# Attention layer 1: two transposes of running maxima moved among the score matmuls, and the last two weight sums of a unit put on four column groups

## The chip, the cores and the metric

The kernel runs on one core of a Trainium2 chip. A core has five engines with one instruction queue each: PE (TensorE, matmuls and transposes into PSUM), DVE (VectorE), ACT (ScalarE), POOL (GpSimd) and SP, which here only issues DMAs. An engine executes its queue in order; engines wait for each other through semaphores. The metric is the device time of one execution in microseconds (us), the median of three runs.

## The reference

Two layers run one after the other on x of shape (2, 256, 64, 64). Layer 0 is a gated attention with heads of 16 channels. The change touches only layer 1, a plain attention over 4096 positions with four heads of 64 channels:

```python
qkv = jnp.einsum('oc,bchw->bohw', w_qkv, x) + b_qkv[None, :, None, None]
qkv = qkv.reshape(b, HEADS, 3 * head_dim, h * w)
q, k, v = jnp.split(qkv, 3, axis=2)
scale = 1.0 / jnp.sqrt(jnp.asarray(head_dim, x.dtype))
attn = jax.nn.softmax(jnp.einsum('bhdn,bhdm->bhnm', q, k) * scale, axis=-1)
out = jnp.einsum('bhnm,bhdm->bhnd', attn, v).reshape(b, c, h, w)
return jnp.einsum('oc,bchw->bohw', w_out, out) + b_out[None, :, None, None] + x
```

Everything is float32. The softmax needs, for each query, the maximum of its scores, the exponentials and their sum.

## The kernel before

Layer 1 is cut into 32 units (b, g, j): image b, pair of heads g, block j of 512 queries. A unit has 32 chunks m of 128 keys; one chunk of scores for both heads is a tile of 128 partitions (keys) by 1024 elements (two heads, 512 queries each). The chunks form two groups n of 16, and each group has its own maxima.

The main loop goes by steps t, two chunks per step and 16 steps per unit. In this text the steps of a unit are numbered 0 to 15 by the unit whose scores they compute. The scores of a chunk are kept raw in a ring of 26 buffers and used 11 or 12 steps later, when the maxima of its group are known. So one step holds, for two new chunks and two old ones:

- PE: `score` (line 888), two matmuls a chunk into one of two PSUM pair buffers; `gather` (1030), the product of the old chunks' weights with the values; and one of several side jobs: a quarter of a projection (812, 835), transposes of maxima (`turn_max`, 918), sums of weights (1043 and 1060), transposes of results (1085).
- DVE: the running maximum `rmax` (905) of each new chunk, and `shift` (977), which adds the negative maximum to each old chunk.
- ACT: a copy of the new scores into the ring (906, after the `rmax` of the same chunk), which frees the PSUM pair buffer for the score two chunks later; the exponential of the old chunks (`weigh`, 989); copies of side results out of PSUM.
- POOL: `acc` (999 and 1001), the sum over chunks of the weights, one addition of 128x1024 per chunk for 30 of 32 chunks. Chunk 11 of each group is shifted on POOL (966), not on DVE. A ring buffer comes free for a new chunk only when POOL has added the old one: the copy of chunk 9 of a unit takes the buffer of chunk 15 of the unit before, 26 chunks back.

`seq` records the order of the code as the order of each engine's queue, so the order of the calls in the loop at line 1364 is the order on the engines. Side jobs are hung on a step with a place, by `at(step, place, job)`, and called by `hung(step, place)`. The order of a step was: both scores, exponential of one old chunk, "start", "early", `keep` of the first new chunk (rmax and copy), shift and exponential of an old chunk, "early end", `keep` of the second, both gathers, "late", "late end", shift of the next old chunk, "end".

All PSUM side results share one bank, which `misc` hands out (tag `misc`, one buffer): who takes it waits until its last reader is done.

The parts that the change touches:

- Folding the maxima, at step 8 for the first group and at step 0 of the next unit for the second. `turn_max(u, n, k)` transposes the running maxima of head k (four 128x128 transposes) into the `misc` bank, and `fold` reduces them on DVE (935, `negs`) and sends them by DMA. Head 0 was turned "early" and folded "early end"; head 1 was turned "late" and folded "late end". Both heads use the one `misc` bank, so the second transpose needs the first reduction to be over.
- Projected values: `store_values` copies a half out of the `misc` bank on ACT at step 8 ("start"); in the last eight units `output` does the like (1200).
- The weights of chunks 30 and 31 are not added by POOL. `gather` sums them on PE at step 11 of the next unit, by matmuls with a block of ones (1043). Both chunks went to the same two column groups (partitions 64 and 96 of the tile `sum`), accumulating. At step 12 `total` (1060) added the two POOL sums, the first on partitions 0 and 32, the second again on 64 and 96. `keep_total` at step 13 copied the tile out (1068) and turned it to one value per query by four small DMAs to DRAM and one back; `add_sums` at step 15 combined the groups on POOL (1151, 1152), and `factors` the reciprocals.

Of the kernel before, what the change touches and what calls it, by code (L numbers as in the profile page):

```python
# [8 lines left out]
F32 = mybir.dt.float32  # L9
# [5 lines left out]
P = 128  # L15
# [5 lines left out]
D1 = 64  # L21
# [5 lines left out]
def conv_attention_kernel(  # L27
# [743 lines left out]
    with (  # L771
# [23 lines left out]
            (u, n): dram.tile([2, NB], F32, tag=f"neg_{u}_{n}", name=f"neg_{u[0]}{u[1]}{u[2]}_{n}")  # L795
            for u in units for n in range(NG)
        }
        sum1 = {
            u: dram.tile([NG * 2, NB], F32, tag="sum_{}_{}_{}".format(*u), name=f"sum_{u}")
            for u in units  # L800
        }
        first, begun, late = {}, set(), {}


# [217 lines left out]
        def gather(t):  # L1022
            u = b, g, j = units[t // NM]
            m = t % NM
            n = m // GS
            if m % GS == 0:
                avs1[u, n] = psv.tile([P, NB], F32, tag="av", name=f"av1_{b}_{g}_{j}_{n}")
            v = vs[b, g, m // PB]
            for k in range(2):
                seq(nc.tensor.matmul(  # L1030
                    avs1[u, n][k * D1 : (k + 1) * D1, :], v[:, m % PB, k, :], raws[t][:, k, :],
                    start=(m % GS == 0), stop=(m % GS == GS - 1),
                ))
            if on_tensor(t) and t % 2 == 1 and t != 2 * END - 1:
                late_sums((t - 1, t) if on_tensor(t - 1) else (None, t))
            elif t == 2 * END - 2:
                late_sums((t, t + 1))
            if m == NM - 1 and u != units[-1]:
                srows[u] = misc(f"sum1_{b}_{g}_{j}")
                for i in (t - 1, t):  # L1040
                    for k in range(2):
                        r = D1 * (NG - 1) + 32 * k
                        seq(nc.tensor.matmul(
                            srows[u][r : r + 32, :], ones[:, :32], raws[i][:, k, :],
                            start=(i < t), stop=False, skip_group_check=True,
                        ))
            raws.pop(t - 2, None)
            if m % GS == GS - 1:
                a = l1.tile([P, NB], F32, tag="avs", name=f"avs1_{b}_{g}_{j}_{n}")
                seq(nc.scalar.copy(a, avs1.pop((u, n))))  # L1050
                avs1[u, n] = a

        def total(u):


            b, g, j = u
            for n in range(NG):
                for k in range(2):
                    r = D1 * n + 32 * k
                    seq(nc.tensor.matmul(  # L1060
                        srows[u][r : r + 32, :], ones[:, :32], accs[u, n][:, k, :],
                        start=(n < NG - 1), stop=True, skip_group_check=True,
                    ))

        def keep_total(u):
            b, g, j = u
            row = l1.tile([P, NB], F32, tag="kv", name=f"srow_{b}_{g}_{j}")
            seq(nc.scalar.copy(
                row.rearrange("p (a m i) -> p a i m", m=P, i=2),
                srows[u].rearrange("p (a i m) -> p a i m", m=P, i=2),  # L1070
            ))
            for m in range(2 * NG):
                nc.sync.dma_start(out=sum1[u][m : m + 1, :], in_=row[32 * m : 32 * m + 1, :])
            s = small.tile([P, NG, 2, PB], F32, tag="sums1", name=f"sums1_{b}_{g}_{j}")
            nc.sync.dma_start(
                out=s.rearrange("p n k (a i) -> p (n k a) i", i=2),
                in_=sum1[u].rearrange("m (a p i) -> p (m a) i", p=P, i=2),
            )
            srows[u] = s
            seq(nc.scalar.activation(losts[u], losts[u], AF.Exp, scale=D1**-0.5))  # L1080

        def turned(a, name):
# [66 lines left out]
        def add_sums(u):  # L1149
            s, lost = srows[u], losts[u]  # L1150
            seq(nc.gpsimd.tensor_tensor(s[:, 0], s[:, 0], lost, ALU.mult))
            seq(nc.gpsimd.tensor_tensor(s[:, 1], s[:, 1], s[:, 0], ALU.add))

        def factors(u):
# [66 lines left out]

        for n, u in enumerate(units):
            b, g, j = u
            t0 = n * US
            if n > 0:
                at(t0 - 9, "start", lambda u=u, b=b, j=j: fetch(("q", u), x1[b][j]))
                for q in range(4):
                    at(t0 - (3, 3, 2, 2)[q], "late", lambda u=u, q=q: next_queries(u, q))  # L1230
                at(t0 - 2, "start", lambda u=u: keep_next_queries(u, 0))
                at(t0 - 1, "start", lambda u=u: keep_next_queries(u, 1))
            if n < len(units) - NJ:
                to = (*units[n + NJ][:2], j)
                at(max(t0 - 1, 0), "start", lambda to=to: fetch(("kv", *to), x1[to[0]][to[2]]))
                for q in range(4):
                    at(t0 + 2 + q, "late", lambda to=to, q=q: next_keys(*to, q))
                    at(t0 + (6, 7, 9, 10)[q], "late", lambda to=to, q=q: next_values(*to, q))
                at(t0 + 6, "start", lambda to=to: store_keys(*to))
                for i, step in enumerate((t0 + 8, t0 + 11)):  # L1240
                    at(step, "start", lambda to=to, i=i: store_values(*to, i))

                t1 = (n // NJ * NJ + NJ - 1) * US
                at(t1 + 2 * j + 2, "start", lambda to=to: load_keys(*to))
                at(t1 + 2 * j + 3 + LAG, "start", lambda to=to: load_values(*to))
            for k in range(NG):
                t1 = t0 + (k + 1) * GS // 2
                places = ("early", "early" if (u, k) == (units[-1], NG - 1) else "late")
                for i, place in enumerate(places):
                    at(t1, place, lambda u=u, k=k, i=i: turn_max(u, k, i))  # L1250
                    at(t1, f"{place} end", lambda u=u, k=k, i=i: fold(u, k, i))
                at(t1 + 2, "end", lambda u=u, k=k: place_shift(u, k))
            t1 = t0 + US + GS // 2
            if u != units[-1]:
                at(t1 + 4, "late", lambda u=u: total(u))
                at(t1 + 5, "start", lambda u=u: keep_total(u))
                at(t1 + 1, "late", lambda u=u: lose(u))
                at(t1 + 7, "late end", lambda u=u: add_sums(u))
                at(t1 + 8, "end", lambda u=u: factors(u))
                for place, k in (("early", 1), ("late", 0)):  # L1260
                    at(t1 + 9, place, lambda u=u, k=k: turn_sums(u, k))
                    at(t1 + 9, f"{place} end", lambda u=u, k=k: rows(u, k))
            else:
                at(END + 1, "late", lambda u=u: last_lost(u))
                at(END + 4, "early", lambda u=u: late_sums((None, None)))
                at(END + 4, "early end", lambda u=u: keep_late(0))
                at(END + 5, "early", lambda u=u: turn_late(0))
                at(END + 5, "early end", lambda u=u: add_late(u, 0))
                at(END + 6, "early", lambda u=u: turn_sums(u, 0))
                at(END + 6, "early end", lambda u=u: first_rows(u))  # L1270
                at(END + LAG, "late", lambda u=u: turn_late(1))
                at(END + LAG, "late", lambda u=u: add_late(u, 1))
                at(END + LAG, "late", lambda u=u: turn_sums(u, 1))
                at(END + LAG, "late", lambda u=u: last_rows(u))
            if n >= len(units) - NJ:
                b0 = B - 2
                at(t0 - 1, "start", lambda b0=b0, j=j: fetch_output(b0, j))
                for o in range(CC):
                    for q in range(4):
                        step = t0 + ((2, 3, 4, 5), (6, 7, 9, 10))[o][q]  # L1280
                        at(step, "late", lambda b0=b0, j=j, o=o, q=q: project_out(b0, j, o, q))
                at(t0 + 6, "start", lambda b0=b0, j=j: output(b0, j, 0, 2))
                for part, step in enumerate((t0 + 8, t0 + 11)):
                    at(step, "start", lambda b0=b0, j=j, part=part: output(b0, j, 1, part))

# [76 lines left out]
        for t in range(max(t for t, _ in extras) + 1):  # L1364
            inside, behind = 0 <= t < END, 0 <= t - LAG < END
            pair = (2 * t, 2 * t + 1)
            scores = [score(c) for c in pair] if inside else []
            if 0 <= t - LAG - 1 < END:
                weigh(pair[1] - 2 * LAG - 2)
            hung(t, "start")  # L1370
            hung(t, "early")
            if inside:
                keep(pair[0], scores[0])
# [83 lines left out]
```

## Time and profile before

| | value |
|---|---|
| median of 3 runs | 4638.63 us (4638.25 to 4638.99) |
| the profiled execution, its own time | 4640.95 us |
| its span, first to last instruction | 4639.2 us |
| PE, DVE, ACT, POOL busy in the span | 97%, 83%, 74%, 54% |
| one unit of layer 1, 3123.58 to 3202.48 us | 78.90 us |
| in it PE, DVE, ACT, POOL busy | 75.83, 73.99, 69.75, 74.19 us |
| mean granted TensorE clock | 0.996 |

Layer 1 begins near 2070 us; its units follow each other at 78.9 us (79.0 in the last eight). In a unit four engines are each busy for 88 to 96% of the time, so no single share tells what bounds it. The page counts time to the modelled end of a matmul, which overlaps the next; the distance from one start to the next start on an engine is the time that an instruction takes of its queue, and the prediction goes by that.

The timeline has one line per run of equal instructions: start in us, length in us, engine, line, operation, output and inputs, shapes, how many, and in square brackets the idle time before it and what ended it. Each fp32 matmul shows as two instructions, so a chunk of scores is "x4".

### The profile page before, as it was taken

Reading aid. Unit: us, or ns where it says so; the run is one execution under the profiler, and the core shown is the slowest. Engines: PE = TensorE matmul, PEld = TensorE weight load, DVE = VectorE, ACT = ScalarE, POOL = GpSimd, SP = SyncE. Lnnn points to the kernel's source line nnn. Section 1 sums busy time; section 2 is a strip of 40 time slices with the busy share of each in tenths; the row PEclk is TensorE's granted clock in tenths of the full one; section 3 lists DMA queues with packets and bytes.
Section 4 is the critical chain, followed back from the end, with each engine's and each line's share of the span. In section 5 each row is a group of like instructions: output and inputs, shape, how many; then the busy total and the mean of one; then the engine's idle time right before and its main releaser. Section 6 shows DMA issues by size and latency. Waiting matters only on the chain. (4 is left out here: it accounts for less than half of the span.)

```text
span 4639.2 us, 73122 instructions
## 1 busy us (share of the span) xinstructions
PE 4499.0 (97%) x28490; PEld 1511.6 (33%) x28490; DVE 3833.4 (83%) x4443; ACT 3439.9 (74%) x4588; POOL 2514.8 (54%) x1307
## 2 busy tenths in 40 slices
PE   8999999999999999999999999999999999999998
PEld 3433333333333333333333333333333333323332
DVE  6777777777777777529999999999999999999997
ACT  3266666666666666668888888888888888888885
POOL 5300000000000000008999999999999999999995
PEclk9999999999999999999999999999999999999999
DMA  3100000000000000121111221111211112111213
GB/s 101 39 4 20 20 20 15 15 15 15 15 15 15 15 13 13 33 75 40 35 42 35 55 56 39 37 40 42 71 42 36 39 33 62 51 53 37 53 40 112
DMA packets 190475, 174.84 MB, mean 38 GB/s; under 512 B 120232, under 2 KB 121064, under 8 KB 190128
## 3 DMA queue, kind: packets, MB, share of 16 engines
q1 hardware_dynamic: 188272, 169.58, 13.2%
q8 instruction: 223, 3.65, 0.3%
q14 instruction: 124, 1.02, 0.1%
q10 hardware_dynamic: 1856, 0.59, 0.1%
HBM read 127.65 MB, written 42.48 MB: 37 GB/s over the span
## 5 line engine op out<-in xcount | busy, mean ns | idle before, releaser
L1001 POOL TENSOR_TENSOR acc<-acc,raw 128x1024 f32<-128x1024 f32 x821 | 1950.4, 2376 | 80.1 <-ACT raw L989 30.7
L402 DVE TENSOR_REDUCE mx<-a 128x1 f32<-128x512 f32 x2048 | 1315.5, 686 | 449.9 <-PE a L398 448.8
L439 ACT ACTIVATE p<-s 128x512 f32<-128x512 f32 x2048 | 1108.3, 595 | 702.5 <-PE a L398 367.6
L905 DVE TENSOR_TENSOR rmax<-s,rmax 128x1024 f32<-128x1024 f32 x960 | 1171.6, 1220 | 99.7 <-PE s L888 89.6
L436 PE MATMUL s<-q,kT 32*128 32x512 f32 x4096 | 1218.8, 640 | 0.0
L888 PE MATMUL s<-q,k 64*128 64x512 f32 x4096 | 1120.3, 637 | 98.1 <-ACT raw L906 93.2
L906 ACT COPY raw<-s 128x1024 f32<-128x1024 f32 x1024 | 1035.6, 1011 | 240.8 <-DVE rmax L905 163.5
L977 DVE TENSOR_TENSOR raw<-raw,shift 128x1024 f32<-128x1024 f32 x961 | 1160.7, 1212 | 3.3 <-ACT shift L959 1.8
L989 ACT ACTIVATE raw<-raw 128x1024 f32<-128x1024 f32 x1024 | 1084.9, 1060 | 62.8 <-DVE raw L977 27.7
L398 PE MATMUL a<-kT,q 32*128 32x512 f32 x4096 | 1129.8, 643 | 1.4 <-DVE mx L402 1.3
L1030 PE MATMUL av<-raw,v 128*64 128x512 f32 x4096 | 1007.4, 607 | 4.2 <-ACT raw L989 2.5
L451 PE MATMUL av<-p,v 128*32 128x256 f32 (+1 forms) x7904 | 650.1, 399 | 0.6 <-ACT avs L465 0.6
L501 POOL TENSOR_TENSOR f<-f,dyn 128x16 f32<-128x16 f32 x15 | 3.3, 221 | 1028.2 <-DVE f L500 1028.2
L888 PEld LDWEIGHTS s<-q,k 64*128 64x128 f32 x4096 | 316.8, 185 | 678.7 <-ACT raw L906 487.0
L436 PEld LDWEIGHTS s<-q,kT 32*128 32x128 f32 x4096 | 397.7, 183 | 426.3 <-issue 392.1
L1030 PEld LDWEIGHTS av<-raw,v 128*64 128x64 f32 x4096 | 242.4, 136 | 650.8 <-issue 476.4
L451 PEld LDWEIGHTS av<-p,v 128*32 128x32 f32 x7904 | 157.7, 108 | 751.5 <-issue 737.3
L552 POOL TENSOR_SCALAR res<-res 128x1024 f32<-128x1024 f32 x16 | 16.7, 1044 | 660.3 <-ACT res L551 660.3
L398 PEld LDWEIGHTS a<-kT,q 32*128 32x128 f32 x4096 | 305.2, 184 | 31.4 <-DVE mx L402 18.2
L999 POOL TENSOR_TENSOR acc<-raw,raw 128x1024 f32<-128x1024 f32 x64 | 152.1, 2376 | 60.9 <-ACT raw L989 60.3
L966 POOL TENSOR_TENSOR raw<-raw,row 128x1024 f32<-128x1024 f32 x63 | 151.7, 2407 | 37.9 <-DMA row<-neg 37.9
L935 DVE TENSOR_REDUCE negs<-rt 128x4 f32<-128x512 f32 x126 | 87.0, 690 | 58.8 <-PE rt L918 58.8
(338 smaller groups left out, 1913.5 us busy)
## 6 DMA issues: line engine op xcount, KB each, us to landing
row<-neg SPq DMA_DIRECT2D x64, 512.0 KB
x<-in_x_dram SPq DMA_DIRECT2D x16, 512.0 KB
res<-in_x_dram SPq DMA_DIRECT2D x16, 512.0 KB
x<-res SPq DMA_DIRECT2D x16, 512.0 KB
att<-rows SPq DMA_DIRECT2D x62, 128.0 KB
kd<-k1s SPq DMA_DIRECT2D x24, 256.0 KB
vd<-v1s SPq DMA_DIRECT2D x24, 256.0 KB
k<-kd SPq DMA_DIRECT2D x24, 256.0 KB
```

The costliest lines, as they stand in the source:

```text
L398: seq(nc.tensor.matmul(ps, qs0[u][r, bass.ts(i, P)], kTs[b][r, bass.ts(m, NB)], start=True, stop=True,))
L402: seq(nc.vector.tensor_reduce(mxs[u][:, i * H + h, m : m + 1], ps, AX.X, ALU.max))
L436: seq(nc.tensor.matmul(ps, kTs[b][r, bass.ts(m, P)], qs0[u][r, :], start=True, stop=True))
L439: seq(nc.scalar.activation(pt[:, k, :], ps, AF.Exp, scale=D0**-0.5))
L451: seq(nc.tensor.matmul(avs[u][32 * h : 32 * h + 32, cols], vs0[b][:, m, 32 * h : 32 * h + 32], pts[t, h // 2][:, h % 2, cols], start=(m == ...
L888: seq(nc.tensor.matmul(ps[:, k, :], ks[b, g, m // PB][r, bass.ts(m % PB, P)], qs1[u][r, :], start=True, stop=True,))
L905: seq(nc.vector.tensor_tensor(rmax[u, n], ps, before, ALU.max))
L906: seq(nc.scalar.copy(raw, ps))
L977: seq(nc.vector.tensor_tensor(raws[t], raws[t], shifts[u, t % NM // GS], ALU.add))
L989: seq(nc.scalar.activation(p, p, AF.Exp, scale=D1**-0.5))
L1001: seq(nc.gpsimd.tensor_tensor(accs[u, n], accs[u, n], p, ALU.add))
L1030: seq(nc.tensor.matmul(avs1[u, n][k * D1 : (k + 1) * D1, :], v[:, m % PB, k, :], raws[t][:, k, :], start=(m % GS == 0), stop=(m % GS == GS ...
```

## The change

Three things are altered, all in layer 1.

1. In a step, the second `score` is now recorded after the exponential of the old chunk and the places "first", "start" and "between". Head 0 of the maxima is turned at "between", that is between the two scores, and folded at "early end" as before; head 1 is turned at "early end" too, right after that, which on PE is behind the second score and ahead of the gathers, and folded at "late end". The fold of the last unit's second group stays as it was. On PE a folding step goes from score, score, transposes 0, gather, gather, transposes 1 to score, transposes 0, score, transposes 1, gather, gather.
2. The first half of `store_values` (and of `output`) moves to "first", on ACT ahead of the exponential of the old chunk.
3. The matmuls over chunks 30 and 31 write four column groups of a tile of their own, `csum`, none accumulating on another. It has its own way out: `keep_chunks` at step 12 copies it on ACT and sends it through DRAM, five DMAs on SP's queue as for `sum`; `total` takes the `misc` bank anew afterwards; `add_sums` adds both of its parts on POOL, two more operations.

```diff
@@ -795,10 +795,14 @@
             (u, n): dram.tile([2, NB], F32, tag=f"neg_{u}_{n}", name=f"neg_{u[0]}{u[1]}{u[2]}_{n}")
             for u in units for n in range(NG)
         }
-        sum1 = {
-            u: dram.tile([NG * 2, NB], F32, tag="sum_{}_{}_{}".format(*u), name=f"sum_{u}")
-            for u in units
-        }
+        sum1, csum1 = (
+            {
+                u: dram.tile([4, NB], F32, tag="{}_{}_{}_{}".format(s, *u), name=f"{s}_{u}")
+                for u in units
+            }
+            for s in ("sum", "csum")
+        )
+        csums = {}
         first, begun, late = {}, set(), {}
@@ -1036,13 +1040,14 @@
             elif t == 2 * END - 2:
                 late_sums((t, t + 1))
             if m == NM - 1 and u != units[-1]:
-                srows[u] = misc(f"sum1_{b}_{g}_{j}")
-                for i in (t - 1, t):
+                csums[u] = misc(f"csum1_{b}_{g}_{j}")
+                for i in range(2):
                     for k in range(2):
-                        r = D1 * (NG - 1) + 32 * k
+                        r = D1 * i + 32 * k
                         seq(nc.tensor.matmul(
-                            srows[u][r : r + 32, :], ones[:, :32], raws[i][:, k, :],
-                            start=(i < t), stop=False, skip_group_check=True,
+                            csums[u][r : r + 32, :], ones[:, :32], raws[t - 1 + i][:, k, :],
+                            start=True, stop=True,
                         ))
             raws.pop(t - 2, None)
             if m % GS == GS - 1:
@@ -1054,29 +1059,36 @@
             b, g, j = u
+            srows[u] = misc(f"sum1_{b}_{g}_{j}")
             for n in range(NG):
                 for k in range(2):
                     r = D1 * n + 32 * k
                     seq(nc.tensor.matmul(
                         srows[u][r : r + 32, :], ones[:, :32], accs[u, n][:, k, :],
-                        start=(n < NG - 1), stop=True, skip_group_check=True,
+                        start=True, stop=True,
                     ))
-        def keep_total(u):
-            b, g, j = u
-            row = l1.tile([P, NB], F32, tag="kv", name=f"srow_{b}_{g}_{j}")
+        def keep_rows(ps, to, tag, name):
+            row = l1.tile([P, NB], F32, tag="kv", name=f"srow_{name}")
             seq(nc.scalar.copy(
                 row.rearrange("p (a m i) -> p a i m", m=P, i=2),
-                srows[u].rearrange("p (a i m) -> p a i m", m=P, i=2),
+                ps.rearrange("p (a i m) -> p a i m", m=P, i=2),
             ))
-            for m in range(2 * NG):
-                nc.sync.dma_start(out=sum1[u][m : m + 1, :], in_=row[32 * m : 32 * m + 1, :])
-            s = small.tile([P, NG, 2, PB], F32, tag="sums1", name=f"sums1_{b}_{g}_{j}")
+            for m in range(4):
+                nc.sync.dma_start(out=to[m : m + 1, :], in_=row[32 * m : 32 * m + 1, :])
+            s = small.tile([P, 2, 2, PB], F32, tag=tag, name=f"sums1_{name}")
             nc.sync.dma_start(
                 out=s.rearrange("p n k (a i) -> p (n k a) i", i=2),
-                in_=sum1[u].rearrange("m (a p i) -> p (m a) i", p=P, i=2),
+                in_=to.rearrange("m (a p i) -> p (m a) i", p=P, i=2),
             )
-            srows[u] = s
+            return s
+        def keep_chunks(u):
+            csums[u] = keep_rows(csums[u], csum1[u], "csums", "c_{}_{}_{}".format(*u))
+        def keep_total(u):
+            srows[u] = keep_rows(srows[u], sum1[u], "sums1", "{}_{}_{}".format(*u))
             seq(nc.scalar.activation(losts[u], losts[u], AF.Exp, scale=D1**-0.5))
         def turned(a, name):
@@ -1149,6 +1161,9 @@
         def add_sums(u):
             s, lost = srows[u], losts[u]
             seq(nc.gpsimd.tensor_tensor(s[:, 0], s[:, 0], lost, ALU.mult))
+            c = csums.pop(u)
+            seq(nc.gpsimd.tensor_tensor(s[:, 0], s[:, 0], c[:, 0], ALU.add))
+            seq(nc.gpsimd.tensor_tensor(s[:, 1], s[:, 1], c[:, 1], ALU.add))
             seq(nc.gpsimd.tensor_tensor(s[:, 1], s[:, 1], s[:, 0], ALU.add))
         def factors(u):
@@ -1212,6 +1227,7 @@
         def fetch_output(b, j):
             fetch(("xo", b, j), x1[b][j], "xo", 1, l1)
             fetch(("ao", b, j), att[b][:, bass.ts(j, NB)], "ao", 1, l1)
@@ -1237,21 +1253,25 @@
                     at(t0 + 2 + q, "late", lambda to=to, q=q: next_keys(*to, q))
                     at(t0 + (6, 7, 9, 10)[q], "late", lambda to=to, q=q: next_values(*to, q))
                 at(t0 + 6, "start", lambda to=to: store_keys(*to))
-                for i, step in enumerate((t0 + 8, t0 + 11)):
-                    at(step, "start", lambda to=to, i=i: store_values(*to, i))
+                for i, (step, place) in enumerate(((t0 + 8, "first"), (t0 + 11, "start"))):
+                    at(step, place, lambda to=to, i=i: store_values(*to, i))
                 t1 = (n // NJ * NJ + NJ - 1) * US
                 at(t1 + 2 * j + 2, "start", lambda to=to: load_keys(*to))
                 at(t1 + 2 * j + 3 + LAG, "start", lambda to=to: load_values(*to))
             for k in range(NG):
                 t1 = t0 + (k + 1) * GS // 2
-                places = ("early", "early" if (u, k) == (units[-1], NG - 1) else "late")
-                for i, place in enumerate(places):
-                    at(t1, place, lambda u=u, k=k, i=i: turn_max(u, k, i))
-                    at(t1, f"{place} end", lambda u=u, k=k, i=i: fold(u, k, i))
+                if (u, k) == (units[-1], NG - 1):
+                    places = ("early", "early end", "early", "early end")
+                else:
+                    places = ("between", "early end", "early end", "late end")
+                for i in range(2):
+                    at(t1, places[2 * i], lambda u=u, k=k, i=i: turn_max(u, k, i))
+                    at(t1, places[2 * i + 1], lambda u=u, k=k, i=i: fold(u, k, i))
                 at(t1 + 2, "end", lambda u=u, k=k: place_shift(u, k))
             t1 = t0 + US + GS // 2
             if u != units[-1]:
+                at(t1 + 4, "start", lambda u=u: keep_chunks(u))
                 at(t1 + 4, "late", lambda u=u: total(u))
                 at(t1 + 5, "start", lambda u=u: keep_total(u))
                 at(t1 + 1, "late", lambda u=u: lose(u))
@@ -1280,8 +1300,8 @@
                         step = t0 + ((2, 3, 4, 5), (6, 7, 9, 10))[o][q]
                         at(step, "late", lambda b0=b0, j=j, o=o, q=q: project_out(b0, j, o, q))
                 at(t0 + 6, "start", lambda b0=b0, j=j: output(b0, j, 0, 2))
-                for part, step in enumerate((t0 + 8, t0 + 11)):
-                    at(step, "start", lambda b0=b0, j=j, part=part: output(b0, j, 1, part))
+                for part, (step, place) in enumerate(((t0 + 8, "first"), (t0 + 11, "start"))):
+                    at(step, place, lambda b0=b0, j=j, part=part: output(b0, j, 1, part))
@@ -1364,10 +1384,14 @@
         for t in range(max(t for t, _ in extras) + 1):
             inside, behind = 0 <= t < END, 0 <= t - LAG < END
             pair = (2 * t, 2 * t + 1)
-            scores = [score(c) for c in pair] if inside else []
+            scores = [score(pair[0])] if inside else []
+            hung(t, "first")
             if 0 <= t - LAG - 1 < END:
                 weigh(pair[1] - 2 * LAG - 2)
             hung(t, "start")
+            hung(t, "between")
+            if inside:
+                scores.append(score(pair[1]))
             hung(t, "early")
             if inside:
                 keep(pair[0], scores[0])
```

## The prediction

> **What bounds the kernel now.** I read the busy shares, then the distance between units (78.90 us nearly throughout), then the timeline of one unit, to see which engine has no gap in which step. First step 8, where the first group's maxima are folded, PE's lines and then DVE's (its first score is at 3104.35):
>
> ```profile
> 3105.65 1.13 PE L888 MATMUL s<-q,k 64*128 64x512 f32 x4 [0.16 <-ACT raw L906]
> 3107.02 0.66 PE L918 MATMUL rt<-ident,rmax 128*128 128x128 f32 x4 [0.25 <-ACT v1s L844]
> 3107.61 1.94 PE L1030 MATMUL av<-raw,v 128*64 128x512 f32 x8
> 3109.48 0.66 PE L918 MATMUL rt<-ident,rmax 128*128 128x128 f32 x4
> 3110.06 1.99 PE L888 MATMUL s<-q,k 64*128 64x512 f32 x8
> ...
> 3105.53 1.22 DVE L905 TENSOR_TENSOR rmax<-s,rmax 128x1024 f32<-128x1024 f32 x1
> 3106.67 1.21 DVE L977 TENSOR_TENSOR raw<-raw,shift 128x1024 f32<-128x1024 f32 x1
> 3107.80 0.69 DVE L935 TENSOR_REDUCE negs<-rt 128x4 f32<-128x512 f32 x1
> ...
> 3111.24 1.23 DVE L905 TENSOR_TENSOR rmax<-s,rmax 128x1024 f32<-128x1024 f32 x1 [0.38 <-PE s L888]
> ```
>
> DVE starts an operation every 1.13 to 1.14 us and enters the step without a gap; here it stands still only for PE, before 3111.24. From there to step 11 it runs again nearly without gaps, so what delays that `rmax` delays the unit. The gathers (1.87 from start to start) lie between the two transposes and cover the first reduction. Next, steps 11 to 13:
>
> ```profile
> 3123.58 1.91 PE L1043 MATMUL sum<-raw,ones 128*32 128x512 f32 x8
> 3125.42 1.99 PE L888 MATMUL s<-q,k 64*128 64x512 f32 x8
> 3127.34 1.94 PE L1030 MATMUL av<-raw,v 128*64 128x512 f32 x8
> 3129.21 1.07 PE L1060 MATMUL sum<-acc,ones 128*32 128x512 f32 x8
> 3130.20 2.17 PE L888 MATMUL s<-q,k 64*128 64x512 f32 x8
> ...
> 3126.60 1.23 DVE L905 TENSOR_TENSOR rmax<-s,rmax 128x1024 f32<-128x1024 f32 x1 [1.55 <-PE s L888]
> ...
> 3127.08 2.39 POOL L999 TENSOR_TENSOR acc<-raw,raw 128x1024 f32<-128x1024 f32 x1 [2.26 <-ACT raw L989]
> ```
>
> Here PE is the bound: DVE waits 1.55 for the scores behind the sums. POOL also waits for ACT, then has no gap from step 13 to past step 5 of the next unit. Where that chain arrives:
>
> ```profile
> 3167.13 2.39 POOL L1001 TENSOR_TENSOR acc<-acc,raw 128x1024 f32<-128x1024 f32 x1
> ...
> 3168.32 1.22 DVE L905 TENSOR_TENSOR rmax<-s,rmax 128x1024 f32<-128x1024 f32 x1
> ...
> 3169.63 1.02 ACT L906 COPY raw<-s 128x1024 f32<-128x1024 f32 x1
> ```
>
> This copy is chunk 9's, at step 5. It needs the `rmax` (ends 3169.54) and the ring buffer that POOL's addition of chunk 15 frees (ends 3169.52). Other units show the same tie within 0.05. So three chains take turns: PE at 11 to 14, DVE at 15 to 11, and POOL, with no margin, at 5.
>
> **Step 8: plus 0.94 a unit.** DVE's work up to the first reduction is not moved: `rmax` 3105.53, shift 3106.67, reduction 3107.80 to 3108.49. On ACT the copy of v1s (3106.62, 0.35 long, behind the exponential at 3105.65) now comes ahead of the exponential: about 3105.53 (0.95 behind the copy of scores at 3104.58) to 3105.88. Transposes 0 go at about 3105.93 instead of 3107.02, and take 0.59 of the queue; the second score goes at 3106.52 and PE is free at 3107.58 (1.06). Transposes 1 need the `misc` bank, so they wait for the reduction until 3108.49 + 0.05 (the v1s copy ended 3106.97, its waiter began 3107.02): 3108.54. Behind them on PE are queued both gathers, the projection and the next scores. Gathers 3108.54 + 0.59 = 3109.13; next scores 3109.13 + 1.87 = 3111.00 against 3110.06. The next `rmax` moves by the same 0.94. The cover that is gone is the gathers': PE idles 0.96 ahead of transposes 1. The earlier second reduction gains nothing, since DVE then waits for the scores. In the unit at 3026 the same working gives 1.04, my upper end. The lower end is 0, if the reduction were over when PE arrives; the rows speak for 0.94. Had the v1s copy stayed behind the exponential, transposes 0 would go 1.09 later, and still be ready for the reduction at 3107.80; so this move costs or gains nothing, covered by that wait. In the last eight units the copy is `output`'s, 0.46 instead of 0.35, under the same cover.
>
> In the trace gathers followed by a projection of the same 128*64 shape take 1.77 to the next start, and 1.87 followed by 128*128 transposes, so a change of shape shows as 0.10. The Trainium skill, in "TensorEngine Tiling (Array Packing)", Tiling Modes, under Key Properties, says that changing the tiling mode drains the array, which speaks against putting 128*128 transposes between 64*128 scores: a folding step then has five changes instead of four. If each counted, 63 folds by 0.10 would add 6 us; I count nothing, because the extra one lies in the 0.96 of idle.
>
> **Step 0: plus 0.13 a unit.** The step has no `rmax` for its first chunk, so its reduction comes earlier.
>
> ```profile
> 3144.39 2.34 DVE L977 TENSOR_TENSOR raw<-raw,shift 128x1024 f32<-128x1024 f32 x2
> 3147.38 0.69 DVE L935 TENSOR_REDUCE negs<-rt 128x4 f32<-128x512 f32 x1 [0.65 <-PE rt L918]
> ...
> 3145.63 1.13 PE L888 MATMUL s<-q,k 64*128 64x512 f32 x4 [0.72 <-ACT raw L906]
> ...
> 3147.25 0.20 POOL L1151 TENSOR_TENSOR sums<-sums,lost 128x8 f32<-128x8 f32 x1
> 3147.53 0.20 POOL L1152 TENSOR_TENSOR sums<-sums 128x8 f32<-128x8 f32 x1
> ```
>
> Transposes 0 now fill PE's 0.72 of idle. The reduction goes when DVE is free, 3144.39 + 2 x 1.13 = 3146.65, and ends 3147.34. Transposes 1 go at 3147.39, gathers 3147.98, next scores 3149.85. Before, transposes 0 were at 3146.69 (right behind the score, 1.06), gathers 3147.28, transposes 1 3149.14, scores 3149.73. The stall of 0.72 comes back as a wait for the reduction; 0.13 more. Ends: minus 0.59, if nothing waited there and only the filled transposes counted, and plus 0.3, if the two shifts took their full 1.21 each.
>
> **Step 11: minus 0.85 a unit.** The eight instructions of 1043 take 3125.42 - 3123.58 = 1.84 of the queue on two column groups, those of 1060 take 0.99 on four (3129.21 to the next scores at 3130.20). `csum` writes four, so 0.85 is saved where PE is the bound; DVE's wait falls to 0.70. Scores, `rmax` and copies follow from step 12 on by the same 0.85. The added ACT copy (0.51 of its queue, as 1068) lies where ACT waited 0.91 for the `rmax`; with `rmax` 0.85 earlier, ACT ends about 0.08 behind and recovers by its next waits. `total` now waits for that copy, which ends near 3127.5, while PE comes to it at 3128.36: nothing. Ends: 0.63, if ACT sets the pace as it does for POOL below, and 0.85.
>
> **POOL: 0.52 more at step 5.** POOL's first addition of a unit waits for an exponential that ACT reaches in its own time (3127.08), so POOL gains nothing there; the second gains about 0.63. The two extra additions of 128x8 cost 0.28 (from 1151 to 1152) and 0.16 (from 1152 to the next start, 3147.69): 0.44. At step 5 POOL is thus only 0.19 earlier than before, while DVE and PE would be 0.85 - 0.13 = 0.72 earlier. Since they were tied, the copy of chunk 9 waits for POOL by about 0.5, and through it the next score. Behind that copy on ACT are the exponentials and copies, on PE the gathers. Ends: 0, if there is margin that I don't see, and 0.65, if both additions cost 0.28.
>
> SP's five added issues a unit (four and one, 0.3 to 0.4 us each by the DMA lines) lie in a queue that waits for its sources most of the time; their result is used at step 15, three steps later. Nothing, and about 2 us a unit if they held back POOL's chain.
>
> **Sum.** 31 x (0.94 + 0.13 - 0.85) = 6.8 us, and POOL 30 x 0.52 = 15.6: together 22.4. Against the profiled span 4639.2 that is 4661.6; the profiled execution itself took 4640.95, 2.3 above the median. On the median, 4638.63 + 22.4 = **4661.0 us**. A measurement can tell 0.2% from no change, 9.3 us.
>
> **Rivals.** (a) *POOL has margin*: then only 6.8 us, 4645.4, no change by that bound. For it: POOL's part rests on one tie. Against: the tie repeats in every unit that I read. (b) *Faster: step 8 gives its delay back in steps 10 and 11.* PE waits there for ACT, 0.47 and some 0.30 a unit; if late scores only ate those waits, step 8 would cost 0.17, and with margin on POOL the change is 31 x (0.17 + 0.13 - 0.85) = -17, 4621.6. Without POOL's tie the unit gets shorter as soon as more than 0.22 of the 0.94 comes back. Against it: those waits of PE come from DVE's pace, and DVE starts later by the same 0.94. (c) *Heavier*: 1.04 and 0.3 at the folds, 0.63 saved and POOL 0.65: 31 x 0.71 + 30 x 0.65 = 41.5, 4680. (d) *The sums do not run side by side*: the 0.85 is not there and POOL comes 0.44 later, so a unit gets 0.94 + 0.44 longer: 31 x 1.38 = 43, 4681.
>
> **Chances.** Forecast 0.55, (a) 0.17, (b) 0.13, (c) and (d) together 0.10, the rest 0.05 near no change. Likeliest: 4661.0. Range 4638 to 4676: it takes in (a), leaves out (b) and the far part of (c) and (d). The low ends of both folds need a reduction that is over early, which DVE's gapless rows exclude, but for (b). Slower by over 0.2%: 0.68; within: 0.19; faster: 0.13.
>
> **What would show it.** In the profile after: at step 8 an idle of about 0.95 ahead of the second transposes, ended by `negs`, and DVE waiting about 2 us before the next `rmax`; at step 0 about 0.7 the same way; `csum` with 0.99 to the next start and DVE's wait at step 12 near 0.7; the copy of chunk 9 ended by POOL; a unit of 79.6 us. A unit under 78.9, or no wait of PE for `negs`, would make the forecast wrong.

## The result and the profile after

The changed kernel takes **4657.53 us** (median of 6 runs, 4656.64 to 4658.49), the kernel before 4638.58 (6 runs, 4638.25 to 4638.99): a ratio of 1.0041 (1.0028 to 1.0054), 18.95 us slower. The forecast was 4661.0, so 22.4 slower. The profiled span is 4654.7 us against 4639.2, at a granted clock of 0.997.

The page's busy times, from part 1, of the kernel before and of the changed kernel:

```profile
PE 4499.0 (97%) x28490; PEld 1511.6 (33%) x28490; DVE 3833.4 (83%) x4443; ACT 3439.9 (74%) x4588; POOL 2514.8 (54%) x1307
PE 4470.4 (96%) x28490; PEld 1503.6 (32%) x28490; DVE 3828.8 (82%) x4443; ACT 3445.9 (74%) x4619; POOL 2525.4 (54%) x1369
```

TensorE is busy for 4470.4 us, 28.6 less than before; most of that are the sums over chunks 30 and 31, busy for 1.06 us a unit instead of 1.91. The kernel is slower all the same, so what it lost is idle time on TensorE, and the page doesn't say where; the timeline of one unit does. First step 8, PE and then DVE (start, length, engine, line, operation, and in brackets the idle time just ahead with what ended it):

```profile
3109.82 1.13 PE L892 MATMUL s<-q,k 64*128 64x512 f32 x4
3111.26 0.66 PE L922 MATMUL rt<-ident,rmax 128*128 128x128 f32 x4 [0.31 <-ACT v1s L848]
3111.85 1.13 PE L892 MATMUL s<-q,k 64*128 64x512 f32 x4
3114.01 0.66 PE L922 MATMUL rt<-ident,rmax 128*128 128x128 f32 x4 [1.03 <-DVE negs L939]
3114.59 1.94 PE L1034 MATMUL av<-raw,v 128*64 128x512 f32 x8
3116.46 1.99 PE L892 MATMUL s<-q,k 64*128 64x512 f32 x8
...
3113.27 0.68 DVE L939 TENSOR_REDUCE negs<-rt 128x4 f32<-128x512 f32 x1
3113.87 1.21 DVE L909 TENSOR_TENSOR rmax<-s,rmax 128x1024 f32<-128x1024 f32 x1
3115.00 0.68 DVE L939 TENSOR_REDUCE negs<-rt 128x4 f32<-128x512 f32 x1
3117.64 1.23 DVE L909 TENSOR_TENSOR rmax<-s,rmax 128x1024 f32<-128x1024 f32 x1 [1.96 <-PE s L892]
```

PE has its second score behind it at 3112.9 and then stands for 1.03, until the first reduction has ended (3113.27 + 0.68 = 3113.95) and has freed the one `misc` bank. The gathers, which used to cover this reduction, go only after the second transposes. From the step's first scores to the next step's it is 3116.46 - 3109.82 = 6.64 us, against 5.71 before (3104.35 to 3110.06). DVE pays on the other side, 1.96 of idle ahead of the next `rmax`, where it had 0.38.

Step 0, the same way, from the last `rmax` of step 15 to the first scores of step 1:

```profile
3069.44 1.22 DVE L909 TENSOR_TENSOR rmax<-s,rmax 128x1024 f32<-128x1024 f32 x1
3070.58 2.34 DVE L981 TENSOR_TENSOR raw<-raw,shift 128x1024 f32<-128x1024 f32 x2
3070.85 0.66 PE L922 MATMUL rt<-ident,rmax 128*128 128x128 f32 x4
3071.81 1.13 PE L892 MATMUL s<-q,k 64*128 64x512 f32 x4 [0.31 <-ACT raw L910]
3072.84 0.68 DVE L939 TENSOR_REDUCE negs<-rt 128x4 f32<-128x512 f32 x1
3073.57 0.66 PE L922 MATMUL rt<-ident,rmax 128*128 128x128 f32 x4 [0.63 <-DVE negs L939]
3076.03 1.99 PE L892 MATMUL s<-q,k 64*128 64x512 f32 x8
```

The same two ends before:

```profile
3143.26 1.22 DVE L905 TENSOR_TENSOR rmax<-s,rmax 128x1024 f32<-128x1024 f32 x1
3149.73 1.99 PE L888 MATMUL s<-q,k 64*128 64x512 f32 x8
```

The transposes fill the idle ahead of the second score, 0.31 of it being left, and 0.63 comes back as a wait for the reduction. From end to end it is 3076.03 - 3069.44 = 6.59 us against 6.47.

The sums at step 11, with the two lines that show how early DVE and POOL are behind them:

```profile
3050.45 1.06 PE L1048 MATMUL csum<-raw,ones 128*32 128x512 f32 x8
3051.44 2.16 PE L892 MATMUL s<-q,k 64*128 64x512 f32 x8
3052.62 1.23 DVE L909 TENSOR_TENSOR rmax<-s,rmax 128x1024 f32<-128x1024 f32 x1 [0.71 <-PE s L892]
3053.94 2.39 POOL L1003 TENSOR_TENSOR acc<-raw,raw 128x1024 f32<-128x1024 f32 x1 [3.12 <-ACT raw L993]
```

On four column groups the eight instructions hold the queue for 0.99 instead of 1.84. POOL's first addition starts 3.49 behind the start of the sums, where it was 3.50 (3127.08 - 3123.58): nothing gained there. Last the place that the prediction calls step 5 of the next unit, where POOL's chain ends in the copy of chunk 9. (By the numbering of the steps chunk 9 belongs to step 4. Its copy comes as the scores of step 5 begin, and "step 5" means this moment below.)

```profile
3093.80 2.38 POOL L1005 TENSOR_TENSOR acc<-acc,raw 128x1024 f32<-128x1024 f32 x1
3094.61 1.22 DVE L909 TENSOR_TENSOR rmax<-s,rmax 128x1024 f32<-128x1024 f32 x1
3096.22 1.01 ACT L910 COPY raw<-s 128x1024 f32<-128x1024 f32 x1 [0.43 <-POOL acc L1005]
```

`rmax` is done at 3095.83, POOL's addition at 3096.18; the copy starts at 3096.22, behind POOL. The waits of PE over most of layer 1, from 2240 to 4560 us:

```profile
PE s L892 <- ACT raw L910: 73.0, 202, 0.9
PE rt L922 <- DVE negs L939: 47.4, 58, 1.0
PE rt L922 <- ACT v1s L848: 6.5, 21, 0.3
```

Each line has engine and line, what it waited for, us in total, how many times, and the longest. The second line is new. 47.4 us over 58 folds is a mix of the 1.03 and the 0.63.

A unit is now 79.53 us long (sums at 3050.45, the next at 3129.98), 0.63 more than 78.90. Read from the start of the sums, each anchor against its place before:

| stretch | before | after | difference |
|---|---|---|---|
| sums to the copy of chunk 9 | 46.05 | 45.77 | -0.28 |
| that copy to the scores of step 8 | 13.63 | 13.60 | -0.03 |
| scores of step 8 to those of step 9 | 5.71 | 6.64 | +0.93 |
| scores of step 9 to the next sums | 13.51 | 13.52 | +0.01 |
| unit | 78.90 | 79.53 | +0.63 |

30 x 0.63 is 18.9 us, the measured difference.

### The profile page after: what moved, and what is told of

Its sections match the earlier page's. It is cut to its first block, busy times and chain, and to the rows that moved or that the text cites. A ratio compares the mean times of both kernels' runs of the same rounds, so it can differ in the third digit from the quotient of the medians.

```text
span 4654.7 us, 73549 instructions
## 1 busy us (share of the span) xinstructions
PE 4470.4 (96%) x28490; PEld 1503.6 (32%) x28490; DVE 3828.8 (82%) x4443; ACT 3445.9 (74%) x4619; POOL 2525.4 (54%) x1369
## 5 line engine op out<-in xcount | busy, mean ns | idle before, releaser
L922 PE MATMUL rt<-ident,rmax 128*128 128x128 f32 x504 | 82.6, 287 | 62.6 <-DVE negs L939 50.6
```

## The experiments

Ten kernels ran in three groups, each timed 4 to 11 times beside the kernel before on the same chip, which stood at 4640.06, 4639.19 and 4639.33 us. Gains and losses below are against that time of the own group, and two kernels of different groups are compared by these. The theory to be tested: step 8's fold costs some 0.9 a unit because the gathers no longer cover the first reduction; the sums gain less than 0.85; POOL's two additions take part of that gain away. Rivals: changes of shape on PE, the sums' own trip through memory, a margin on POOL.

### One half at a time

**sums_alone**: the fold's transposes go back, the sums stay as changed.

```diff
-                for i, (step, place) in enumerate(((t0 + 8, "first"), (t0 + 11, "start"))):
+                for i, (step, place) in enumerate(((t0 + 8, "start"), (t0 + 11, "start"))):
...
-                    places = ("between", "early end", "early end", "late end")
+                    places = ("early", "early end", "late", "late end")
```

> The four column groups, the own trip and POOL's two additions, without the moved maxima: both transposes and the copy of the projected values stand where they stood before. Theory (the folds cost, the sums gain, and POOL's chain sets what reaches step 5): in the changed kernel chunk 9's copy comes 0.28 us a unit earlier than before, counted from the sums, because POOL is late; without the moved maxima that 0.28 is the whole change: a unit of 78.62 us, 30 x -0.28 = -8.4, about 4630 us. Rival 1 (POOL does not bind): the sums' gain on the path comes through, 0.69 to 0.85 a unit, 4612 to 4617 us. Rival 2 (the new trip itself costs, the folds cost nothing): 4657 us or more.

Measured 4628.78 us (4627.69 to 4631.76), ratio 0.9976 (0.9967 to 0.9986): 11.3 faster than before, 0.38 a unit. Whatever the trip's issues on SP and the added copy on ACT cost, it is less than the sums save. But 0.38 is not the 0.85 of the queue that the sums save; the next group of runs says who keeps the rest.

**maxima_alone**: the kernel before with the new places of the transposes and the scores split around them, its sums untouched.

```diff
...
+                    places = ("between", "early end", "early end", "late end")
...
-            scores = [score(c) for c in pair] if inside else []
+            scores = [score(pair[0])] if inside else []
+            hung(t, "first")
...
+            hung(t, "between")
+            if inside:
+                scores.append(score(pair[1]))
```

> The moved maxima and the score behind them, on the kernel before, whose sums are as they were: Theory: step 8 costs 0.92 us a unit and step 0 0.12, and POOL, which has no new work, gives 0.07 of margin at step 5: a unit of 78.90 + 0.92 + 0.05 to 0.12 = 79.87 to 79.94 us, 4668 to 4671 us. Rival 1 (late scores are made up in steps 10 and 11): below 4645 us. Rival 2 (the folds cost nothing, the new trip does): 4638 us.

Measured 4671.69 (4670.6 to 4673.45), ratio 1.0068 (1.0056 to 1.0081): 31.6 slower, 1.02 a unit over 31 folding units, against 0.93 + 0.12 = 1.05 from the two steps' lines. The wait view of PE from 2300 to 4500 us has the cause:

```profile
PE rt L918 <- DVE negs L935: 42.0, 55, 1.1
```

Alone the two halves make -11.3 and +31.6, together 20.3; the whole change measures 18.95. The two effects nearly add up.

### Is it the cover, or the shapes?

**first_reduction_early**: the changed kernel, with the first reduction put ahead of the shift of DVE's next chunk instead of behind it. All matmuls stay in the order of the change.

```diff
-                    places = ("between", "early end", "early end", "late end")
+                    places = ("between", "folded", "early end", "late end")
...
                 keep(pair[0], scores[0])
+            hung(t, "folded")
```

> The changed kernel with one thing altered: the reduction of head 0 is put on DVE ahead of the shift of the old chunk instead of behind it; PE's order is the changed one. Theory (PE waits ahead of transposes 1 for the reduction because both use one PSUM bank): the reduction begins 1.13 us sooner, the wait of 1.03 at step 8 falls to below 0.1, and the unit loses 0.92: 79.52 - 0.92 = 78.60 us, about 4630 us, with POOL's chain as the bound at step 5. At step 0 the wait of 0.63 goes too, which POOL hides. Rival (what costs is the place of the transposes between other shapes on PE, or the gathers behind them): 4657 us as in the changed kernel.

Measured 4627.26 (4625.29 to 4627.88), ratio 0.9971 (0.996 to 0.9983). PE's timeline in step 8:

```profile
3020.18 1.13 PE L892 MATMUL s<-q,k 64*128 64x512 f32 x4
3021.62 0.66 PE L922 MATMUL rt<-ident,rmax 128*128 128x128 f32 x4 [0.31 <-ACT v1s L848]
3022.20 1.13 PE L892 MATMUL s<-q,k 64*128 64x512 f32 x4
3023.26 0.66 PE L922 MATMUL rt<-ident,rmax 128*128 128x128 f32 x4
3023.85 1.94 PE L1034 MATMUL av<-raw,v 128*64 128x512 f32 x8
3025.71 2.01 PE L892 MATMUL s<-q,k 64*128 64x512 f32 x8
```

The order is that of the changed kernel, line for line, but no wait stands ahead of the second transposes, and the step takes 5.53 instead of 6.64. So the price was the reduction's lateness. The Trainium skill ("TensorEngine Tiling (Array Packing)", Key Properties) says that changing the tiling mode drains the array. In this place no cost of that shows: by the prediction's count the step has five changes of shape instead of four, and it takes 5.53 us, 0.31 of them a wait for ACT, where it took 5.71 with 0.41 of such waits.

**second_turn_late**: the changed kernel, with the second transposes back behind the gathers, the first ones still between the scores.

```diff
-                    places = ("between", "early end", "early end", "late end")
+                    places = ("between", "early end", "late", "late end")
```

> The changed kernel with the second transposes back behind the gathers; the first stay between the scores. Theory (the gathers were the cover of the reduction): the wait for the reduction is gone at both folds, as it was when the reduction was put earlier, and POOL's chain binds at step 5: a unit of 78.6 us, 4627 to 4630 us. At step 0 the scores come 0.58 us sooner, which POOL hides. Rival (what helped before was the earlier reduction on DVE, not PE's cover): nearer to the changed kernel's 4657 us.

Measured 4626.35 (4624.71 to 4628.33), ratio 0.9973 (0.9962 to 0.9983). The gathers cover the reduction again, and the loss is gone. Both cures stop at about 4627, near sums_alone: something else sets the time there. The copy of chunk 9, in second_turn_late:

```profile
3002.24 2.37 POOL L1005 TENSOR_TENSOR acc<-acc,raw 128x1024 f32<-128x1024 f32 x1
3002.32 1.22 DVE L909 TENSOR_TENSOR rmax<-s,rmax 128x1024 f32<-128x1024 f32 x1
3004.64 1.01 ACT L910 COPY raw<-s 128x1024 f32<-128x1024 f32 x1 [1.15 <-POOL acc L1005]
```

Its `rmax` is done at 3003.54, and the copy waits another 1.10 us for POOL's addition, which ends at 3004.61.

### What keeps the rest of the sums' gain

**additions_on_dve**: the two extra additions of 128x8 go from POOL to DVE, just ahead of the reciprocal.

```diff
-            c = csums.pop(u)
-            seq(nc.gpsimd.tensor_tensor(s[:, 0], s[:, 0], c[:, 0], ALU.add))
-            seq(nc.gpsimd.tensor_tensor(s[:, 1], s[:, 1], c[:, 1], ALU.add))
...
+            s, c = srows.pop(u), csums.pop(u)
+            seq(nc.vector.tensor_tensor(c[:, 0], c[:, 0], c[:, 1], ALU.add))
+            seq(nc.vector.tensor_tensor(s[:, 1], s[:, 1], c[:, 0], ALU.add))
...
```

> The changed kernel with the two additions of the chunks' own sums on DVE, next to the reciprocal at the end of step 0, where DVE waits over 1 us for scores, instead of on POOL. Theory (POOL's chain ties at step 5): POOL gets there 0.44 us a unit sooner, DVE's own chain binds then, at 0.57 ahead of before instead of 0.28: a unit of 79.52 - 0.29 = 79.23 us, about 4649 us. Rival (POOL has margin, its additions cost nothing): 4657 us, no change against the changed kernel.

Measured 4699.84 (4699.74 to 4702.08), ratio 1.013 (1.0115 to 1.0146): 59.8 slower than before, and so 41 worse than the change, where 8 better was expected. The timeline has DVE and then POOL at these additions:

```profile
3092.49 0.77 DVE L1171 TENSOR_TENSOR sums_c<-sums_c 128x8 f32<-128x8 f32 x1
3093.35 2.34 DVE L1172 TENSOR_TENSOR sums<-sums,sums_c 128x8 f32<-128x8 f32 x1
3095.72 0.20 DVE L1173 RECIPROCAL f<-sums 128x8 f32<-128x8 f32 x1
...
3090.86 4.80 POOL L1005 TENSOR_TENSOR acc<-acc,raw 128x1024 f32<-128x1024 f32 x2
```

Two additions of eight elements a partition took 0.77 and 2.34 us, the reciprocal of the same size 0.20. They end at 3093.26 and 3095.69. POOL runs two additions back to back in that time, the first to 3093.23 and the second to 3095.66. In 30 of the 31 units in the trace each of the two on DVE ends 0.02 to 0.03 us behind the end of a POOL addition: they seem to have stood until POOL's running instruction was over. The expectation priced them far too low. The run says nothing on POOL's share, for DVE spent 3.2 us a unit on the two.

**one_reduce_changed_folds**: both results land in one tile, and one reduction on DVE, which reads a single operand, makes the sum; POOL keeps only the multiplication. The folds stay as changed.

```diff
-            s = small.tile([P, 2, 2, PB], F32, tag=tag, name=f"sums1_{name}")
...
+            csums[u] = small.tile([P, 4, 2, PB], F32, tag="sums1", name="sums1_{}_{}_{}".format(*u))
+            keep_rows(ps, csum1[u], csums[u][:, 2:4], "c_{}_{}_{}".format(*u))
...
-            seq(nc.gpsimd.tensor_tensor(s[:, 1], s[:, 1], s[:, 0], ALU.add))
...
+            seq(nc.vector.tensor_reduce(
+                f[:, 1], srows.pop(u).rearrange("p m k i -> p k i m"), AX.X, ALU.add
+            ))
```

> The changed kernel, folds as changed, with the sums and the chunks' own sums in one tile, added by one reduction on DVE (one SBUF operand) ahead of the reciprocal; POOL keeps only the product with lost, one operation of 128x8 instead of four. Theory (POOL's chain ties at step 5; what went wrong with the additions on DVE is that an operation with two SBUF operands stood until POOL's running addition was over, 0.77 and 2.34 us for 128x8): the reduction takes about 0.2 us, POOL reaches step 5 some 0.6 us sooner, DVE's chain binds 0.29 earlier: a unit of 79.23 us, about 4648 us. Rival 1 (POOL has margin at step 5): 4657 us. Rival 2 (any small operation on DVE there stands behind POOL): 4680 us or more.

Measured 4651.01 (4649.48 to 4652.07), ratio 1.0025 (1.0016 to 1.0035). The reduction is short:

```profile
3076.12 0.20 DVE L1170 TENSOR_REDUCE f<-sums 128x8 f32<-128x32 f32 x1
```

It is 11.8 slower than before, 7.1 better than the change: with three small POOL instructions gone, some 0.23 a unit comes back. The 11.8 that are left are about what the folds cost beyond the 0.69 a unit that the sums gain in the next run: 31 x (1.05 - 0.69) = 11.2.

**sums_one_reduce**: the same one reduction with the folds of before, so sums_alone without POOL's additions. The edit against sums_alone is the one above.

> The four column groups with their own trip and one reduction on DVE instead of POOL's additions; the folds stand as before the change. Theory: POOL reaches step 5 some 0.9 us a unit sooner and binds no more, so the sums' gain on PE and DVE comes through as it was measured in the changed kernel at step 15, 0.69: a unit of 78.21 us, 4639.2 - 31 x 0.69 = 4618 us. If the whole of the 0.85 came through: 4613 us. Rival (POOL's chain is not what took the gain): 4629 us, as with the sums alone.

Measured 4617.98 (4617.48 to 4620.76), ratio 0.9957 (0.9943 to 0.997): 21.35 faster, 0.69 a unit over 31 units. The start of the sums and the last `rmax` of step 15:

```profile
3113.99 1.07 PE L1048 MATMUL csum<-raw,ones 128*32 128x512 f32 x8
3132.97 1.22 DVE L909 TENSOR_TENSOR rmax<-s,rmax 128x1024 f32<-128x1024 f32 x1
```

They are 18.98 apart, 0.70 less than before (3143.26 - 3123.58 = 19.68); in the changed kernel it is 18.99. So the sums on four column groups are worth 0.69 a unit, of which POOL's extra instructions keep 21.35 - 11.28 = 10.1 us, 0.32 a unit.

**two_more_on_pool**: the kernel before, with two spare additions of 128x8 a unit on POOL, into a tile that nobody reads.

```diff
+            spare = small.tile([P, 2, PB], F32, tag="spare", name="spare_{}_{}_{}".format(*u))
+            for i in range(2):
+                seq(nc.gpsimd.tensor_tensor(spare, s[:, 0], lost, ALU.add))
```

> The kernel before with two more additions of 128x8 on POOL in add_sums, into a tile that nobody reads, of the kind that the change adds; nothing else. Theory (POOL's chain ties with DVE's at step 5, with 0.07 us of margin): 0.44 less 0.07 is 0.37 us a unit, 30 x 0.37 = 11, about 4650 us, and the copy of chunk 9 is released by POOL. Rival (POOL has margin in the kernel before and binds only where the sums run faster): 4639 us.

Measured 4646.59 (4645.18 to 4647.82), ratio 1.0015 (1.0007 to 1.0024): 7.3 slower, between the two expectations. ACT's timeline at step 5 shows the wait that the kernel before didn't have:

```profile
3093.28 1.01 ACT L906 COPY raw<-s 128x1024 f32<-128x1024 f32 x1 [0.53 <-POOL acc L1001]
```

Behind the start of this unit's sums (3046.85) the copy of chunk 9 comes at 46.43, 0.38 later than before; POOL's addition there ends at 46.40, 0.46 later than the 45.94 of before. (Over 22 units the medians are 0.36 and 0.41 later.) So the tie is real, and its margin is 0.05 to 0.08. Of the 0.38, 0.36 still stands at the scores of step 8 (60.04 against 59.68), and 0.22 behind that step (65.61 against 65.39): PE used to wait 0.16 for ACT between the two scores of step 8, and the delay eats this wait. This unit gets 0.23 longer, and 30 of these make 7 us.

### A version that beats both

**one_reduce_early_reduction** and **one_reduce_second_turn_late** take the one reduction together with either cure of the fold; their edits are those shown above.

> The same single reduction on DVE, together with the fold's reduction ahead of the shift. Theory: no wait of PE for a reduction at the folds, the sums' gain and 0.58 us at step 0 on PE and DVE (1.27 together), and POOL 0.92 us a unit earlier at step 5 than before the change, which is then the bound: a unit of 77.98 us, 30 x -0.92 = -28, about 4611 us. Rival (POOL does not bind at step 5): the 1.27 comes through, about 4600 us. Rival 2 (POOL's additions were never on the path): 4627 us, as with the early reduction alone.

> The single reduction on DVE, with the second transposes behind the gathers instead of an earlier reduction. Theory: the same bounds as with the early reduction, POOL 0.92 us a unit earlier at step 5: 4611 us, or a little more where the second fold comes later. Rival: 4627 us if POOL's additions were never on the path.

Measured 4605.95 (4603.85 to 4607.38), ratio 0.9929 (0.9915 to 0.9942), and **4604.72** (4603.77 to 4606.27), ratio 0.9926 (0.9913 to 0.9938): 33 and 34 us faster than before, 52 and 53 better than the change, and alike within their spreads. They are 5 and 6 us better than expected. No wait of PE for `negs` is left in either. From the waits of ACT, 2240 to 4520 us, of the second:

```profile
ACT raw L910 <- POOL acc L1005: 13.7, 29, 0.7
ACT raw L910 <- POOL acc L1003: 10.3, 29, 0.4
```

Every unit still has copies that wait for POOL. The first transposes between the scores, which looked like a loss, are a gain once the reduction is covered: 34.47 - 21.35 = 13.1 us, together with the earlier copy of the projected values, which no run separates from them.

Where the 5 to 6 us beyond the expectation come from stands in the same trace. The unit whose sums start at 3030.78, PE's step 8 and then the copy of chunk 9:

```profile
3089.44 1.13 PE L892 MATMUL s<-q,k 64*128 64x512 f32 x4
3090.87 0.65 PE L922 MATMUL rt<-ident,rmax 128*128 128x128 f32 x4 [0.31 <-ACT v1s L848]
3091.46 1.13 PE L892 MATMUL s<-q,k 64*128 64x512 f32 x4
3092.52 1.94 PE L1034 MATMUL av<-raw,v 128*64 128x512 f32 x8
3094.39 0.66 PE L922 MATMUL rt<-ident,rmax 128*128 128x128 f32 x4
3094.97 2.01 PE L892 MATMUL s<-q,k 64*128 64x512 f32 x8
...
3075.83 1.01 ACT L910 COPY raw<-s 128x1024 f32<-128x1024 f32 x1 [0.41 <-POOL acc L1005]
```

The copy comes 45.05 behind the start of the sums, 1.00 earlier than before (0.97 in the median of 22 units), where 0.92 was expected. And step 8 takes 5.53 instead of the 5.71 of before: PE waits 0.31 for ACT in it, where it used to wait 0.16 and 0.25. This unit is 77.69 long, 1.21 less than before, and the expectation had counted on POOL's 0.92 alone.

## Why the prediction was right, point by point

- **Step 8, plus 0.94**: 0.93 in the lines of after. The predicted wait ahead of the second transposes, 0.96, was 1.03, ended by `negs`; DVE's idle, "about 2 us", was 1.96. That the gathers' cover is the cause is shown by first_reduction_early and second_turn_late, which take the wait away in two different ways and both lose the delay. Rival (b), that the delay is given back in steps 10 and 11, falls: from step 9 to the sums it is 13.51 before and 13.52 after.
- **Step 0, plus 0.13**: 0.12, with 0.63 of wait for the reduction (the prediction's own rows also give 3149.85 - 3149.73 = 0.12). Both folds together, in maxima_alone, cost 31.6 us where 31 x (0.94 + 0.13) = 33.2 was worked out.
- **Changes of shape, nothing**: held, by the same PE order without the wait.
- **Step 11, minus 0.85**: the sums' own 0.85 on the queue is there (0.99 for 1.84), but 0.69 reaches step 15. From the scores of step 12 to those of 13 it is 4.95 after and 4.78 before, because PE's second score there waits for ACT's copy of earlier scores; the next step gains this back (4.66 for 4.83), the one from 14 to 15 loses it again (4.95 for 4.78), and behind step 15 DVE has no gap to make it up. The prediction let the whole 0.85 follow from step 12 on; the term was mis-sized by 0.16, and its lower end, 0.63 by ACT's pace, was nearer to the truth. Rival (d), sums not side by side, falls.
- **POOL at step 5, 0.52**: the mechanism is shown by sums_one_reduce and two_more_on_pool, and the copy of chunk 9 did end behind POOL. The additions cost 0.45 (0.44 predicted), and POOL's second addition came 0.65 earlier (0.63). The size was wrong, twice over: the tie had a margin of some 0.07, so POOL's addition of chunk 15 comes 0.21 earlier and the copy 0.28 (predicted 0.19); and DVE and PE were only 0.69 - 0.12 = 0.57 ahead, not 0.72. POOL's term is 0.57 - 0.28 = 0.29. (The prediction's own numbers, 0.72 and 0.19, leave 0.53 and not 0.52.)
- **The sum**: 31 x (0.93 + 0.12 - 0.69) = 11.2 and 30 x 0.29 = 8.7 make 19.9, against 6.8 and 15.6 in the prediction and 18.95 measured. The split between the two was off by more than the total: 4.4 us too little on one side, 6.9 too much on the other. That these offset each other is only in part luck. Whatever the sums gain less, POOL has less to take away. But the margin on POOL, which the prediction put at nothing, took off another 2 us, and that this went the right way is luck.
- **Nothing for SP's issues and ACT's added copy**: nothing speaks against it, as sums_one_reduce has the whole 0.69 with both in it, but no run takes them out. The added copy makes the next copy of scores some 0.3 late (the prediction had 0.08), and the copy behind that one is 0.84 earlier than before again.
- **Nothing for the earlier copy of the projected values**: no run tests it alone.
- Rival (a), a margin on POOL large enough to hide the additions (4645.4), falls with one_reduce_changed_folds: taking POOL's small instructions away gives 7 us.

What stays open: what the earlier copy of the projected values is worth by itself, and how much of the two best versions' gain belongs to it.

## What to carry to other kernels

An instruction between two users of one buffer is not free to move: the gathers stood between two transposes that share a bank, and they were what hid the reduction that frees it. Before work is moved forward, ask what it was covering, and move the reduction that frees the buffer first. A gain at one engine's bound comes through only up to the next tie, so look a unit ahead for the chain with no gap, and keep small instructions off it.

## What the runs showed of the hardware

The 128x8 additions on DVE with both operands in SBUF took 0.77 and 2.34 us beside POOL's additions of 2.4 us; the 128x32 reduction with one such operand took 0.20 under the same POOL work, though it differs in its operation too. DVE's `rmax` and shift, which keep one operand in PSUM, show no such stretching (1.21 to 1.23 us each in all of the kernel before).

The Trainium skill, in "SBUF — State Buffer", Who interferes with whom, says that a VectorE instruction with two SBUF inputs contends with a GpSimd instruction that reads SBUF, and that the port pair which they share is an exclusive lock. "GPSIMD Engine Reference", Specifications, names the same contention. The ends at 3093.26 and 3095.69, each 0.03 us or less behind an end of POOL's, agree with it.
